# A mixture of experts with a residual on one core: block products of 4x4 in place of 2x2 in 52 of 72 units

## The chip, the core and the metric

The kernel runs on one core of a Trainium2 chip (trn2). The metric is the device time of one execution in microseconds. All data is fp32.

## The reference

The input x has 16 batch rows of 256 tokens with 256 features. Eight experts and one shared expert each have two matrices up (Wg, Wu, 256 x 1024) and one down (Wd, 1024 x 256). Cut to what matters:

```python
g = jnp.einsum('bsd,edf->ebsf', h, Wg)
u = jnp.einsum('bsd,edf->ebsf', h, Wu)
expert_outs = jnp.einsum('ebsf,efd->ebsd', jax.nn.silu(g) * u, Wd)
expert_output = jnp.einsum('be,ebsd->bsd', gating_probs, expert_outs)
shared = jnp.einsum('bsf,fd->bsd', jax.nn.silu(h @ Sg) * (h @ Su), Sd)
sg = shared_gate_prob[:, :, None]
out = x + (1.0 - sg) * expert_output + sg * shared
```

## The kernel before, in words

**Units.** The work is cut into 72 units: for each expert (the shared one is the ninth), for each half of the 1024 hidden features, for each group g of four batch rows. The loop at the end of the kernel goes through them in this order, so four units follow each other with the same weights. A unit computes a 4x4 grid of hidden blocks (four chunks of 128 features against four batch rows of 256 tokens), for the gate (m = 0) and for the up matrix (m = 1).

**Up.** Products are saved by algebra. Four diagonal blocks are computed plainly (`diagonal`, two weight halves each: the bank D, the copies p and q in SBUF). For each of the six pairs i < j of `PAIRS`, three products give both off-diagonal blocks (`offdiagonal`): one of summed weights and summed x goes to a bank M; GpSimd makes s from q and p (lines 281, 285 on are the helpers `tt` and `stt`); VectorE puts M + s into a bank X as a seed; two more products are added onto X by TensorE. The bank is then consumed: ScalarE applies silu for the gate (line 643), VectorE multiplies the up bank by the gate and by the coefficient of expert and batch row, in one scalar_tensor_tensor per block (`mult`), into a tile h. Summed weights come from `load_base` and `make_pair`, the x sums (xp, xd) were kept in HBM at the start and are loaded again for every unit by SP (line 276).

**Down.** `unit_down` sees the h blocks as 2x2 blocks and uses seven products instead of eight, for each of two feature halves f, which are added in the bank: 14 matmuls of 512 columns. It needs six sums of h by VectorE and two by GpSimd (`sum_`), and sums of Wd from `load_down`. ScalarE copies each of the seven banks dn into a tile ev (line 765), and two DMAs of GpSimd's queue add four and three of these into `total[g]` in HBM (line 780; without adding in the first round, line 778). At the end `load_pieces` and `finish` join the seven pieces of each group into the output, with transposes (line 866); the last unit goes down plainly (`last_down`).

**Order.** Every operation is given to a plan (`add`) with an engine, a length, a rank and the tiles that it makes and uses. A unit takes 12 ranks. `Plan.run` plays the whole program through once when the kernel is built: on each engine the ready operation of lowest rank goes first, tiles are handed out from the list of their tag, and TensorE's operations keep the order of rank within each of two streams (dn or not). The instructions are emitted in the order found, each engine's in a fixed order. PSUM has eight banks: three X, two M, one D, two dn.

## Time and profile before

| what | value |
|---|---|
| median of 3 runs | 2527.62 us (2527.4 to 2527.68) |
| the profiled execution | 2527.65 us |
| its span, first to last instruction | 2525.9 us |
| TensorE busy | 2512.4 us (99%), 9637 matmul records |
| VectorE, ScalarE, GpSimd busy | 1850.4, 788.1, 1718.6 us |
| granted TensorE clock | 1.000 |
| moved by DMA | 425.18 MB, 168 GB/s |

Engines in the profile are PE (TensorE), PEld (its weight loads, which overlap it), DVE (VectorE), ACT (ScalarE), POOL (GpSimd) and SP (SyncE). A group line gives the line of the kernel, engine, operation, written tile <- read tiles, shapes and count; then busy time and mean duration in ns; then the idle time of the engine just before these instructions, and what ended it. L281 is the helper for all two-tensor operations, L545 that for all matmuls, so groups are told apart by their tiles. An fp32 matmul appears as two records. Some 100 us at each end, where tables are made and pieces joined, differ from the steady middle.

### The profile page before, as it was taken

Reading aid. Unit: us, or ns where it says so; the run is one execution under the profiler, and the core shown is the slowest. Engines: PE = TensorE matmul, PEld = TensorE weight load, DVE = VectorE, ACT = ScalarE, POOL = GpSimd, SP = SyncE. Lnnn points to the kernel's source line nnn. Section 1 sums busy time; section 2 is a strip of 40 time slices with the busy share of each in tenths; the row PEclk is TensorE's granted clock in tenths of the full one; section 3 lists DMA queues with packets and bytes.
Section 4 is the critical chain, followed back from the end, with each engine's and each line's share of the span. In section 5 each row is a group of like instructions: output and inputs, shape, how many; then the busy total and the mean of one; then the engine's idle time right before and its main releaser. Section 6 shows DMA issues by size and latency. Waiting matters only on the chain. (4 is left out here: it accounts for less than half of the span.)

```text
span 2525.9 us, 30304 instructions
## 1 busy us (share of the span) xinstructions
PE 2512.4 (99%) x9637; PEld 1817.6 (72%) x9637; DVE 1850.4 (73%) x3246; ACT 788.1 (31%) x1389; POOL 1718.6 (68%) x1652
## 2 busy tenths in 40 slices
PE   9999999999999999999999999999999999999999
PEld 5767777777777777777777777777777777777776
DVE  7896767677776768676767767677767777776787
ACT  3333333333333333333333332333332333332321
POOL 7686767676676767676766667576767676676664
PEclk9999999999999999999999999999999999999999
DMA  7545666566666566666666666665666665666566
GB/s 258 181 163 158 172 161 177 158 167 159 170 161 177 157 155 163 163 169 169 166 159 166 163 169 168 162 155 155 175 161 177 157 167 157 175 160 156 153 191 202
DMA packets 179666, 425.18 MB, mean 168 GB/s; under 512 B 15120, under 2 KB 84256, under 8 KB 170544
## 3 DMA queue, kind: packets, MB, share of 16 engines
q1 hardware_dynamic: 158224, 294.18, 35.3%
q0 software_dynamic: 20224, 128.53, 27.0%
q8 instruction: 76, 1.25, 0.2%
q14 instruction: 86, 0.70, 0.1%
q10 hardware_dynamic: 1056, 0.52, 0.1%
HBM read 276.90 MB, written 146.28 MB: 168 GB/s over the span
## 5 line engine op out<-in xcount | busy, mean ns | idle before, releaser
L281 POOL TENSOR_TENSOR s<-pq,pq 128x512 f32<-128x512 f32 x852 | 1134.6, 1360 | 518.8 <-DVE X L281 507.7
L545 PE MATMUL dn<-h,wd 128*128 128x512 f32 x1988 | 1013.8, 592 | 0.4 <-DVE ev L281 0.4
L545 PE MATMUL X<-xp,wp 128*128 128x256 f32 x3408 | 875.5, 379 | 3.6 <-DVE X L281 3.5
L281 DVE TENSOR_TENSOR X<-M,s 128x512 f32<-128x512 f32 x852 | 588.8, 693 | 365.8 <-PE M L545 236.6
L545 PEld LDWEIGHTS X<-xp,wp 128*128 128x128 f32 x3408 | 646.4, 190 | 238.0 <-issue 123.8
L545 PE MATMUL D<-xd,wb 128*128 128x256 f32 x2272 | 583.8, 379 | 1.1 <-ACT sg L643 0.8
L286 DVE SCALAR_TENSOR_TENSOR h<-X,coef,sg 128x256 f32<-128x256 f32 x852 | 397.9, 478 | 244.5 <-PE X L545 190.2
L545 PEld LDWEIGHTS M<-xp,wp 128*128 128x128 f32 x1704 | 323.4, 190 | 316.8 <-issue 301.3
L545 PE MATMUL M<-xp,wp 128*128 128x256 f32 x1704 | 506.8, 379 | 0.0
L765 ACT COPY ev<-dn 128x512 f32<-128x512 f32 x490 | 287.5, 587 | 635.5 <-PE dn L545 635.5
L545 PEld LDWEIGHTS D<-xd,wb 128*128 128x128 f32 x2272 | 430.9, 190 | 66.2 <-issue 3.0
L281 DVE TENSOR_TENSOR h<-h,h 128x512 f32<-128x512 f32 x426 | 454.7, 1093 | 0.0
L545 PEld LDWEIGHTS dn<-h,wd 128*128 128x128 f32 x1988 | 377.5, 190 | 56.3 <-issue 4.3
L572 ACT COPY pq<-D 128x512 f32<-128x512 f32 x284 | 166.2, 585 | 413.0 <-PE D L545 386.5
L643 ACT ACTIVATE sg<-X 128x512 f32<-128x512 f32 x434 | 258.4, 595 | 115.6 <-PE X L545 106.4
L643 ACT ACTIVATE sg<-D 128x512 f32<-128x512 f32 x142 | 84.8, 597 | 525.5 <-DVE pq L281 525.5
L281 DVE TENSOR_TENSOR pq<-D,pq 128x256 f32<-128x256 f32 x568 | 222.0, 415 | 34.8 <-PE D L545 34.3
L780 POOL DMA_DIRECT2D total<-ev x132 | 116.6, 883 | 186.1 <-ACT ev L765 176.9
L281 POOL TENSOR_TENSOR h<-h,h 128x512 f32<-128x512 f32 x142 | 199.4, 1404 | 49.3 <-PE dn L545 31.6
L281 POOL TENSOR_TENSOR wp<-wb 128x128 f32<-128x128 f32 x216 | 140.4, 685 | 0.0
L286 DVE SCALAR_TENSOR_TENSOR h<-D,coef,sg 128x256 f32<-128x256 f32 x284 | 134.4, 474 | 0.0
L281 POOL TENSOR_TENSOR wp<-wp,wb 128x256 f32<-128x256 f32 x108 | 81.8, 764 | 1.3
(73 smaller groups left out, 470.7 us busy)
## 6 DMA issues: line engine op xcount, KB each, us to landing
xp<-keep_p SPq DMA_DIRECT2D x408, 384.0 KB, 4.0
total<-ev POOLq DMA_DIRECT2D x70, 1024.0 KB, 9.2
xd<-keep_d SPq DMA_DIRECT2D x136, 512.0 KB, 3.5
total<-ev POOLq DMA_DIRECT2D x70, 768.0 KB, 6.7
wb<-in_L_cond_Wg_dram SPq DMA_DIRECT2D x32, 256.0 KB, 9.9
wb<-in_L_cond_Wu_dram SPq DMA_DIRECT2D x32, 256.0 KB, 5.2
wd<-in_L_cond_Wd_dram SPq DMA_DIRECT2D x64, 128.0 KB, 4.0
keep_p<-xp SPq DMA_DIRECT2D x18, 384.0 KB, 3.4
```

Source lines behind the costliest of these rows:

```text
L281: return add(engine, length, rank, lambda: eng.tensor_tensor(o(), a(), b(), op), deps, new, uses)
L286: lambda: nc.vector.scalar_tensor_tensor(o(), a(), c() if callable(c) else c, b(), ALU.mult, op),
L545: lambda: nc.tensor.matmul(o(), w(), mv(), start=start, stop=stop, skip_group_check=onto),
L572: lambda: nc.scalar.copy(p_[:, 2 - 2 * a : 4 - 2 * a, :], bank[:, :, :]), ps,
L643: lambda: nc.scalar.activation(b[:, :, :], bank[:, :, :], AF.Silu), deps, [b], [bank],
L765: lambda ev=ev, at=at, bank=bank: nc.scalar.copy(ev[:, at, :], bank.tile.rearrange("p a t -> p (a t)")),
L780: nc.gpsimd.dma_start(total[g][part], ev[:, 0:k, :], accum_op=ALU.add)
```

## The change

Units 4 to 55 go down by another scheme; the first 4 and the last 16 keep the 2x2 blocks.

- **Down by 4x4 blocks.** The four chunks of features and the four batch rows are treated as in the way up, with Wd as the third matrix (m = 2) of `load_base` and `make_pair`. Each of the six pairs gives three products, and eight more belong to the diagonal: 26 of 256 columns, two in each of 13 banks dn. ScalarE copies the 13 banks to ev, and four DMAs (of 3, 3, 3 and 4 banks) add them to a second set of sums in HBM, `star_total`.
- **What it needs.** For each pair, VectorE multiplies the up bank by the gate in place, ScalarE copies it to h, and VectorE adds both blocks to two places each of a tile acc (8 x 256 columns, one instruction of 1024) and sums the two blocks into g. ScalarE starts acc from the two diagonal tiles. The coefficient now goes into the gate by ScalarE (`scale`, two of 256 columns per gate).
- **Both M products of a pair share one bank** in units 4 to 71; a fourth bank serves X in units 4 to 55.
- **Merge.** In the last 16 units, four `merge` calls, one per group, load the sums of `star_total`, combine them on VectorE with a PSUM bank T and ScalarE, and add four blocks to `total`.
- **Memory handed over.** Three tiles of 8 x 256 serve first as 12 tiles h, in the middle as two acc and one more ev, then as h again (`plan.shift`); likewise wd becomes wp and g, and xio becomes wb.
- **The plan.** Ranks come from a table `RANK`; lengths of VectorE and GpSimd operations that share a port are laid end to end; GpSimd's constant in a length goes from 0.3 to 0.17.

The functions of before live on as `unit_up_w`, `unit_down_w` and `offdiagonal_w` (the last used in the first four units only). The core of the diff:

```diff
@@ -20,11 +20,24 @@
+
+
+RANK = {
+    "first": 4, "q": 2.6, "dc": 2.45, "acc": 0.3, "g": -5.1, "cp": 1.6, "seed": -0.05, "s": -2.0,
+    "lagx": 1.5, "sc": 6.1, "bank": (6.6, 7.1, 8.6, 15.9, 16.4, 16.9, 17.3), "ev": 0.55, "p": 1.8, "xc":
+    0.7, "st": -3.8, "qa": -2.25, "da": 0.25, "ga": -3.25, "pace": 3, "m0": -0.6, "m1": 3.25, "xm": 0,
+    "w": 16, "mp": 8, "m2": 1.5, "ml": 1.75, "lagw": 1.25, "wp": 0.05, "wq": 0.6, "wqa": 0, "wdc": 1.45,
+    "ws": 1.0, "wseed": 0.2, "wxc": 1.7, "to": (-12, 6, -6, -19, -34), "back": (0, 72, -6, -33, 4, 80,
+    20),
+}
+
...
@@ -208,20 +262,50 @@
     banks = tags("X", [P, 2, TB], 3, psum)
-    tags("M", [P, 2, TB], 2, psum)
+    mbanks = tags("M", [P, 2, TB], 2, psum)
     tags("D", [P, 2, TB], 1, psum)
     tags("dn", [P, 2, TB], 2, psum)
+    tags("T", [P, 2, TB], 0, psum)
...
     tags("wb", [P, 4, 2, P], 4)
     tags("wp", [P, 3, P], 16)
-    tags("wd", [P, 2, 7, P], 2)
     tags("pq", [P, 4, TB], 8)
     tags("s", [P, 2, TB], 3)
     tags("sg", [P, 2, TB], 5)
-    tags("h", [P, 2, TB], 22)
+    tags("h", [P, 2, TB], 10)
     tags("ev", [P, 4, 2 * TB], 2)
-    tags("xio", [P, 2, D], 4)
+    tags("g", [P, TB], 0)
...
+        ] if m < 2 else None
         late = 0 if rank < 0 else 8
         ru, rv = ranks or (rank, rank)
+        if m == 2:
+            rows = sources(e)[2][ts(half, 4 * P), :].rearrange("(c p) (k q) -> p c k q", p=P, q=P)
         engine = "ACT" if ranks and m == 0 else "SP"
-        u = load(ru, lambda: b[:, :, 0, :], src[0], 256, [], [b], late=late, engine=engine)
-        v = load(rv, lambda: b[:, :, 1, :], src[1], 256, [], [], [b], late=late)
+        if m == 2:
...
+
+    FIRST, LAST = RANK["first"], NE * NHALF * NG - RANK["w"]
+
+    def star(n):
+
+        return FIRST <= n < LAST
 
...
-    def offdiagonal(n, m, unit, k, rank, pq, pqops, consume):
+    def offdiagonal(n, unit, k, rank, pqs, pqops, consume):
+
+        e, half, g = unit
+        i, j = PAIRS[k]
+        xb, xo = xp[g, k], xpop[g, k]
+        mb = Buf("M", f"M_{n}_{k}")
+        m1 = []
+        for m in range(2):
+            w, wo = pair[m, e, half, k], pairop[m, e, half, k]
+            m1.append(
+                mm(
+                    MM, rank + m / 100, lambda m=m: mb[:, m, :], lambda w=w: w[:, 0, :], lambda: xb[:, 0, :],
+                    m == 0, True, m == 1, [wo, xo[0], *m1], [mb] if m == 0 else [], [w, xb] if m == 0 else [w, xb, mb],
+                )
+            )
+        for m in range(2):
+            w, wo = pair[m, e, half, k], pairop[m, e, half, k]
+            p_, q_ = pqs[m]
+            s, xbank = Buf("s", f"s_{m}_{n}_{k}"), Buf("X", f"X_{m}_{n}_{k}")
+            so = tt(
+                "POOL", rank + m - (RANK["s"] if star(n) else RANK["ws"]), lambda s=s: s[:, :, :], lambda q_=q_: q_[:, i : j + 1 : j - i, :],
+                lambda p_=p_: p_[:, 3 - j : 4 - i : j - i, :], ALU.subtract, 2 * TB, [pqops[m][i], pqops[m][j]],
+                [s], [p_, q_],
+            )
+            seed = tt(
+                "DVE", rank + m + (RANK["seed"] if star(n) else RANK["wseed"]), lambda xbank=xbank: xbank[:, :, :],
+                lambda m=m: mb[:, m : m + 1, :].broadcast_to([P, 2, TB]), lambda s=s: s[:, :, :], ALU.add, 2 * TB,
+                [so, *m1], [xbank], [mb, s], False,
+            )
+            m67 = [
+                mm(
+                    MM, rank + m + (LAGX if star(n) else RANK["lagw"]) + (3 + h) / 8, lambda xbank=xbank, h=h: xbank[:, h, :],
+                    lambda w=w, h=h: w[:, 2 - h, :], lambda h=h: xb[:, 2 - h, :],
+                    False, True, True, [seed, wo, xo[2 - h]], [], [xbank, w, xb],
+                )
+                for h in range(2)
+            ]
+            consume[m](xbank, m67, rank + m + (LAGX + RANK["xc"] if star(n) else RANK["lagw"] + RANK["wxc"]), [(j, i), (i, j)])
...
+        def scale(b, h, block, rank, deps):
+            return add(
+                "ACT", act(TB), rank,
+                lambda: nc.scalar.mul(b[:, h, :], b[:, h, :], coef[:, e, 4 * g + block : 4 * g + block + 1]),
+                [*deps, coef_op], uses=[b],
+            )
+
...
+                ops = [op]
+                if True:
+                    ops = [scale(b, h, block, rank + RANK["sc"], [op]) for h, (_, block) in enumerate(which)]
+                    if key[0] == "d":
...
+            op = add(
+                "DVE", dve(4 * TB), rank, lambda: nc.vector.tensor_tensor(view(), view(), twice(), ALU.add),
+                [*deps, *state["acc"]], [], [acc, *uses], port=port,
+            )
+            state["acc"] = [op]
+
...
+        def start_acc(a, b, deps, rank):
+
+            ops = [
+                add(
+                    "ACT", act(2 * TB), rank, lambda: nc.scalar.mul(acc[:, 2 - 2 * a : 4 - 2 * a, :], b[:, :, :], -1.0),
+                    deps, [acc] if state["new"] else [], [b] if state["new"] else [b, acc],
+                )
+            ]
+            state["new"] = False
...
+                ops.append(
+                    add(
+                        "ACT", act(TB), rank, lambda h=h: nc.scalar.copy(acc[:, 5 + 2 * a - h, :], b[:, h, :]),
+                        [*deps, ops[0]], [], [b, acc],
+                    )
+                )
+            state["acc"] += ops
+
+        def sum_pair(k, rank, b, x, deps, uses, port):
+            gb = Buf("g", f"g_{n}_{k}")
+            op = tt("DVE", rank, lambda: gb[:, :], x, lambda: b[:, 1, :], ALU.add, TB, deps, [gb], [b, *uses], port)
+            pairs[k] = (gb, op)
+
...
+                op = tt(
+                    "DVE", rank, lambda: bank[:, :, :], lambda: bank[:, :, :], lambda: sg[:, :, :], ALU.mult, 2 * TB,
+                    [*deps, *sgops], [], [bank, sg], False,
+                )
+                c = add(
+                    "ACT", act(2 * TB), rank + RANK["cp"], lambda: nc.scalar.copy(b[:, :, :], bank[:, :, :]), [op], [b], [bank]
+                )
+                for h, at in enumerate(which):
+                    hb[at] = (b, h, c)
+                acc_pair(k, rank + RANK["acc"], lambda: bank[:, :, :], [c], [bank], False)
+                sum_pair(k, rank + RANK["g"], b, lambda: bank[:, 0, :], [c], [bank], False)
+
+            return consume
+
+        pqs = {m: (Buf("pq", f"p_{m}_{n}"), Buf("pq", f"q_{m}_{n}")) for m in range(2)}
+        pqops = {0: {}, 1: {}}
+        for d in range(4):
+            a, m = d // 2, d % 2
+            pqops[m].update(
+                diagonal(n, m, unit, a, r0 - W + 3 * d, pqs[m], (gate(f"d{a}"), up(f"d{a}", None))[m])
+            )
+        for k in range(len(PAIRS)):
+            offdiagonal(n, unit, k, r0 + 2 * k, pqs, pqops, (gate(f"o{k}"), up(f"o{k}", k)))
+        return hb, pairs, acc, state
...
+    def unit_down(n, unit, hb, pairs, acc, state):
+        e, half, g = unit
+        r0 = W * n
+        work = []
+        for k, (i, j) in enumerate(PAIRS):
+            w, wo = pair[2, e, half, k], pairop[2, e, half, k]
+            gb, go = pairs[k]
+            hbuf, h, ho = hb[i, j]
+            lo = [ho, hb[j, i][2]]
+            work.append((lambda w=w: w[:, 0, :], wo, lambda gb=gb: gb[:, :], [go], [w, gb]))
+            work.append((lambda w=w: w[:, 1, :], wo, lambda hbuf=hbuf: hbuf[:, 1, :], lo, [w, hbuf]))
+            work.append((lambda w=w: w[:, 2, :], wo, lambda hbuf=hbuf: hbuf[:, 0, :], lo, [w, hbuf]))
+        w, (u, rops) = base[2, e, half], baseop[2, e, half]
+        for at in range(8):
+            i, part = (3 - at, 0) if at < 4 else (at - 4, 1)
+            work.append(
+                (lambda i=i, part=part: w[:, i, part, :], rops[i] if part else u, lambda at=at: acc[:, at, :],
+                 state["acc"], [w, acc])
+            )
+        ev, evops = None, []
+        for b in range(13):
+            part, at = (b // 3, b % 3) if b < 9 else (3, b - 9)
+            rank = r0 + (BANK[b % 3] + 4 * (b // 3) if b < 9 else BANK[b - 6])
+            bank = Buf("dn", f"dn_{n}_{b}")
+            ops = []
+            for h in range(2):
+                wv, wo, mv, mo, bufs = work[2 * b + h]
+                ops.append(
+                    mm(
+                        MM, rank + h / 100, lambda bank=bank, h=h: bank[:, h, :], wv, mv, h == 0, True, h == 1,
+                        [wo, *mo, *ops], [bank] if h == 0 else [], bufs if h == 0 else [*bufs, bank],
+                    )
+                )
+            if at == 0:
+                ev, evops = Buf("ev", f"ev_{n}_{part}"), []
...
+
+                def store(ev=ev, part=part, first=first, k=k):
+                    if first:
+                        nc.gpsimd.dma_start(star_total[g][part], ev[:, 0:k, :])
+                    else:
+                        nc.gpsimd.dma_start(star_total[g][part], ev[:, 0:k, :], accum_op=ALU.add)
+
+                starop[g, part] = add(
+                    "POOL", 0.9, rank + 0.4, store, [*evops, starop.get((g, part))], uses=[ev],
+                    lag=3.0, kb=256 * k * (1 if first else 1.8),
+                )
+
+    BANK = RANK["bank"]
+
...
+    def merge(g, rank):
...
+        view, by, ops = load_sums(g, rank - 2.5)
+        for k, (i, j) in enumerate(PAIRS):
...
+            y = [
+                tt(
+                    "DVE", r, lambda at=at: view(4 + at), lambda at=at: view(4 + at), lambda h=h, bank=bank: bank[:, h, :], op, TB,
+                    [cp, *ops], [], [by, bank], False,
+                )
+                for at, h, op in ((i, 1, ALU.add), (j, 0, ALU.subtract))
+            ]
+            c = tt(
+                "DVE", r, lambda tv=tv: tv(0), lambda tv=tv: tv(0), lambda bank=bank: bank[:, 0, :], ALU.subtract, TB,
+                [cp], [], [t, bank], False,
+            )
+            c = tt(
+                "DVE", r, lambda bank=bank: bank[:, 0, :], lambda tv=tv: tv(0), lambda bank=bank: bank[:, 1, :],
+                ALU.subtract, TB, [c, *y], [], [t, bank], False,
+            )
+            z = stt(
+                r, lambda i=i, j=j: by.tile[:, 3 - j : 4 - i : j - i, :], lambda bank=bank: bank[:, 0:1, :].broadcast_to([P, 2, TB]),
+                -1.0 / d, lambda i=i, j=j: by.tile[:, 3 - j : 4 - i : j - i, :], ALU.add, 2 * TB, [c, *ops], [], [by, bank], False,
+            )
+            ops = [*y, z]
+        for i, t in enumerate(POINTS):
+            if t:
+                ops = [
+                    stt(r, lambda i=i: view(4 + i), lambda i=i: view(3 - i), float(t), lambda i=i: view(4 + i), ALU.add, TB, ops, [], [by]),
...
@@ -931,7 +1350,12 @@
             for k in range(len(PAIRS)):
                 for m in range(2):
                     make_pair(m, e, half, k, r0 + 2 * k + m - (8 if n else -4))
-            load_down(e, half, r0 + W - 8)
+            if not star(n):
+                load_down(e, half, r0 + W - 8)
+            else:
+                load_base(2, e, half, r0 - 3)
+                for k in range(len(PAIRS)):
+                    make_pair(2, e, half, k, r0 + 2 * k + 1)
         if n == end:
...
-        hb, hops = unit_up(n, unit)
+        if star(n):
+            unit_down(n, unit, *unit_up(n, unit))
+            continue
+        for k in range(NG):
+            if n == LAST + int(RANK["m0"] + RANK["m1"] * k + RANK["m2"]):
+                merge(k, W * (LAST + RANK["m0"] + RANK["m1"] * k))
+        hb, hops = unit_up_w(n, unit)
...
+    r0, r1 = W * FIRST, W * LAST
+    bank("M", "X", r0 - 0.01, 1)
+    bank("X", "T", r1 + RANK["xm"], 0)
+    for k, (tag, view) in enumerate((("acc", big_acc[0]), ("acc", big_acc[1]), ("ev", big_ev[2]))):
+        plan.shift([(r0 + RANK["to"][k], "h", big_h[k])], [(tag, [view])])
+        plan.shift([(r1 + (RANK["back"][k] if k != 1 else W * (RANK["m0"] + 3 * RANK["m1"]) + 14), tag, [view])], [("h", big_h[k])])
+    plan.shift([(r0 + RANK["to"][3], "wd", low_wd[:1])], [("wp", low_wp[0]), ("g", low_g[0])])
+    for k in range(2):
+        plan.shift(
+            [(r1 + RANK["back"][3], "wp", low_wp[k]), (r1 + RANK["back"][4 + 2 * k], "g", low_g[k])], [("wd", [low_wd[k]])]
+        )
+    plan.shift([(r0 + RANK["to"][4], "xio", side_xio)], [("wb", side_wb)])
+    plan.shift([(r1 + RANK["back"][5], "wb", side_wb)], [("xio", side_xio)])
     last = {}
```

## The prediction

> **What bounds the kernel now.** I began with the busy time of the whole span and of its steady part, 200 to 2400 us. Columns of the second view: stretch, length, then busy us (and instructions) of each engine, granted clock, DMA share, GB/s.
>
> ```profile
> PE 2512.4 (99%) x9637; PEld 1817.6 (72%) x9637; DVE 1850.4 (73%) x3246; ACT 788.1 (31%) x1389; POOL 1718.6 (68%) x1652
> ```
> ```profile
> 200.00:2400.00 2200.00, 2199.80 (x8425) 1600.33 (x8424) 1582.79 (x2806) 696.00 (x1215) 1497.01 (x1427) 1.00 0.63 164
> ```
>
> TensorE is never idle at full clock. As a busy TensorE need not be at its peak, I then looked at its pace in the timeline (start, duration). What counts is the distance of the starts.
>
> ```profile
> 1200.86 1.03 PE L545 MATMUL D<-xd,wb 128*128 128x256 f32 x4
> 1201.73 1.03 PE L545 MATMUL X<-xp,wp 128*128 128x256 f32 x4
> 1202.59 1.02 PE L545 MATMUL dn<-h,wd 128*128 128x512 f32 x2
> 1203.45 0.59 PE L545 MATMUL M<-xp,wp 128*128 128x256 f32 x2
> ```
>
> Four records of 256 columns take 0.86 us, two of 512 as well. The groups show two records for each fp32 product (3408 X records / 71 units = 48 for 24 products), so a 256-column product costs 0.43 us and a 512-column one 0.86. A unit has 52 small products up (16 D, 12 M, 24 X) and 14 large ones down: 80 in small ones, 80 x 0.43 = 34.4 us. The real period: the accumulating DMAs of total run from 213.3 (unit 4, first) to 2471.9 (unit 69, second), the two of a unit 14.2 apart, so 65 periods are 2244.4 us, 34.53 each. Only 0.13 us a unit is lost; time is the count of products.
>
> Then the groups, for what the other engines pay (idle time left aside; "busy, mean ns"):
>
> ```profile
> L281 DVE TENSOR_TENSOR X<-M,s 128x512 f32<-128x512 f32 x852 | 588.8, 693 | 365.8 <-PE M L545 236.6
> L286 DVE SCALAR_TENSOR_TENSOR h<-X,coef,sg 128x256 f32<-128x256 f32 x852 | 397.9, 478 | 244.5 <-PE X L545 190.2
> L281 DVE TENSOR_TENSOR h<-h,h 128x512 f32<-128x512 f32 x426 | 454.7, 1093 | 0.0
> L281 DVE TENSOR_TENSOR pq<-D,pq 128x256 f32<-128x256 f32 x568 | 222.0, 415 | 34.8 <-PE D L545 34.3
> L765 ACT COPY ev<-dn 128x512 f32<-128x512 f32 x490 | 287.5, 587 | 635.5 <-PE dn L545 635.5
> L281 POOL TENSOR_TENSOR s<-pq,pq 128x512 f32<-128x512 f32 x852 | 1134.6, 1360 | 518.8 <-DVE X L281 507.7
> ```
>
> In the steady part (2200 / 34.53 = 63.7 units) a unit has DVE 24.8, ACT 10.9, POOL 23.5 us busy. Last, what DVE waits for there (total, times, longest) and the DMA queues over the span:
>
> ```profile
> DVE X L281 <- PE M L545: 225.2, 220, 2.3
> DVE h L286 <- PE X L545: 183.0, 161, 1.9
> DVE X L281 <- issue: 54.7, 66, 1.3
> DVE X L281 <- POOL s L281: 41.3, 33, 1.3
> ```
> ```profile
> q1 hardware_dynamic: 158224, 294.18, 35.3%
> q0 software_dynamic: 20224, 128.53, 27.0%
> ```
>
> Most of DVE's idle time is waiting for TensorE, which costs nothing. The fences show where the change can bite: DVE, ACT and the DMA engines.
>
> **What the Trainium skill says.** VectorE: DVE Perf Modes, section "The TRN2 errata — SBUF-src ops pay a fixed extra latency per instruction": an fp32 tensor_tensor takes (N+151)/0.96 ns, 691 at N=512; the trace has 693. It prices N=1024, which the trace lacks, at 1224 ns. SBUF — State Buffer, section "Who interferes with whom": a DVE instruction with two SBUF inputs contends with GpSimd reads, one with at most one does not. The trace agrees: h<-h,h (two SBUF inputs) means 1093 ns, X<-M,s of equal size 693. DMA: Bandwidth & Descriptors, section "Issuing engines are not separate DMA queues": all queues end on the same 16 engines and interleave. The trace agrees: 35.3% and 27.0% make the 0.63 of the steady part.
>
> **TensorE, the gain.** Units 4 to 55 (52 of 72) keep the 52 products up. Down, 13 banks of two 256-column products replace 14 large ones: 26 for 28, 78 x 0.43 = 33.54 us. Two products fewer in 52 units: 52 x 0.86 = **44.7 us**, the ceiling. Weight loads: 156 a unit of 190 ns instead of 132; the X rows already keep a pace of 0.215 us a record with one load each, so I add nothing.
>
> **DVE.** Per 4x4 unit: 12 seeds 8.29 (588.8/71), 8 q 3.13 (222.0/71), 8 products with the gate at 0.693 (nearest row: X<-M,s) 5.54, 6 acc additions of 128x1024 with one PSUM input 7.34 (the page's price; low end four times the slope 693-415=278 ns, 1.11 each; high end 1.97, if they paid the 1093/693 of contention), 6 pair sums at 0.40 2.4 (q row: 0.39 busy, 0.415 mean), weights 106.0/71 x 1.5 = 2.24 (wb and wp rows; three matrices for two). Sum 28.9. Gone are the h sums (6.4) and 16 products with coef. The same rows of before sum to 26.8 where the windows show 24.8, since neighbours overlap; so 26.7 to 28.9 of 33.54, **80 to 86%** after 72%. With acc at its ends the sum is 28.2 to 33.4.
>
> **ACT.** Evictions 13 x 0.587 = 7.6, gates 4.8 (343.2/71), D copies 2.3, 16 scales by coef at 0.417 (the xp scaling row) 6.7, 6 copies of X 3.5, two 512-wide negations at 0.63 (0.417 plus the slope 0.587-0.376) 1.3, four 256-wide copies 1.7. Sum 27.9 of 33.54, **83%** after 31%. Back-to-back ones overlap by 0.1 (gates at 1215.03 and 1215.53 of 0.60 each), so 24 is the low end.
>
> **POOL.** 12 s at 1.27 to 1.36: 15.2 to 16.3; four DMA issues at 0.88: 3.5 instead of 1.8; weight sums (222.2+38.8)/71 x 1.5 = 5.5 instead of 3.7 and 0.8 for wd; h sums (2.8) gone. Sum 24.2 to 25.3, 75%; s queues behind DMA issues that wait for ACT's last eviction of a part, as now (170 us in the steady part), twice as often. The DVE work left has a PSUM input almost throughout, so s should fall to its undisturbed 1.27: nothing added.
>
> **DMA.** Accumulation grows from 7 to 13 blocks of 256 KB a unit. Rate now: 128.53 MB in 27.0% of 2525.9 us, 188 GB/s; 13 x 0.262 MB = 18.1 us. Plain traffic 4.09 MB a unit at 330 GB/s (294.18 in 35.3%): 12.4. Together 30.5 of 33.54, 91%; at the 200 and 355 GB/s of the densest stretches (211 at a share of 1.01 from 1218 us, 373 at 1.05 from 20 us) 28.5, 85%. On SP's queue only the load of down weights changes, one of 512 KB for four of 128 KB. A part is due every 8.4 us, three ev buffers give each 25 us; filling needs about 6, landing 6.7 to 9.2 now. I take no cost.
>
> **The last 16 units and the seams.** Both M products share one bank, the counts are unchanged. Four merges: per merge six pairs of 4 DVE sums at 0.415 and one 512-wide at 0.756 (478+278), three 0.82 and one 1.09: 18 us, in all 72 us of DVE, 4 x 4.4 of ACT, loads of 3.3 MB each, four POOL issues each. What hides them is DVE's idle 34.53-24.8 = 9.7 us a unit, 155 us in 16 units; without that cover they cost up to 72. I take 1.5. At the second seam unit 55 goes down within itself and 56 only in the next period: one stretch has 52 products (22.4 us) against 20.4 of DVE work (8.3+5.6+1.9+3.1+1.5); I take 2, range 0 to 5. The first seam stacks TensorE work instead. Its bank hand-over issues one zero matmul, under 0.5 us.
>
> **Sum.** Against the profiled execution, 2527.65 (span 2525.9 and 1.75 around it; median of the runs 2527.62, so no shift): -44.7, +1.5, +2, and for fuller queues 0.06 us a unit on top of today's 0.13, +3: 2527.65 - 38 = **2490**. What is late next is still TensorE.
>
> **Rivals.** *B, bursts take half.* ACT at 83% delays evictions of the two dn banks (the last four banks of a unit are due within 1.4 ranks, 4 us); TensorE stalls 0.35 to 0.9 us a unit beyond the sum: 2505 to 2533. For it: ACT's load grows 2.5 times; against: evictions need 0.59 of the 0.86 that a bank's products take.
> *C, DVE becomes the bound.* Of its idle 9.7 us, waits not put down to TensorE are about 2.6 us (POOL 69, ACT 41, issue 56 over 63.7 units). New waits arise: each product now waits for ACT's scaling, each acc addition for ACT's copy, and behind a waiting DVE instruction stand seeds for which TensorE waits. With 28.9 busy it decides from 34.53-28.9 = 5.6 us of such idle. At 6.6 a unit takes 35.5: +1 x 52 = 52, so 2580. Against: only 80% busy if neighbours overlap, and seeds lead the X products by 1.5 ranks (4 us).
> *D, the DMA engines become the bound.* Decides from (34.53-12.4)/13 = 1.70 us a block, against 1.39 now; at the 2.5 us between the landings of 1024 and 768 KB (9.2, 6.7) a unit takes 45 us, +540. Against: those landings shared the engines with plain loads.
> *E,* that fewer products don't save, is excluded by the pace.
>
> **Chances.** Forecast, 2480 to 2505: 0.60. B as a gain, 2505 to 2522: 0.12; as no change: 0.06. C 0.16, D 0.06. A run can tell about 0.2%, 5 us. So faster 0.72, same 0.06, slower 0.22. The range runs from the ceiling and a little (2480) into C, to 2545; about 0.16 lies above, little below. The forecast's own range is 2480 to 2505.
>
> **What would show it.** Right: units 33.6 to 33.8 us apart, TensorE 99%, acc additions near 1.22 us, s near 1.27, DVE 80 to 86%. B: weight loads or products into dn waiting for ACT evictions. C: products into X waiting for seeds, TensorE under 97%. D: waits for xp or xd loads, landings of ev over 19 us. I am wrong if 4x4 units exceed 34.2 us.

## The result and the profile after

The changed kernel takes 2538.31 us (median of 5 runs, 2535.15 to 2540.82) against 2527.62: 1.0041 times the time of before, 95% interval 1.0027 to 1.0056. Slower by 0.4%, where 1.5% faster was forecast. The profiled execution took 2535.15 us. Ratios here and below are against the kernel before, timed again on the same chip beside each experiment (2527.62 to 2527.88 us).

First the views that answer to those of before: busy time, the steady stretch (length, busy us and instructions of PE, PEld, DVE, ACT, POOL, then clock, DMA share, GB/s), and TensorE's pace.

```profile
PE 2486.8 (98%) x10885; PEld 2057.6 (81%) x10886; DVE 2051.4 (81%) x3330; ACT 1570.7 (62%) x3185; POOL 1698.7 (67%) x1759
```
```profile
200.00:2400.00 2200.00, 2167.47 (x9641) 1833.25 (x9640) 1778.17 (x2882) 1458.72 (x2969) 1474.54 (x1525) 1.00 0.83 209
```
```profile
1200.85 1.03 PE L640 MATMUL D<-xd,side 128*128 128x256 f32 x4
1201.71 1.03 PE L640 MATMUL X<-xp,wp 128*128 128x256 f32 x4
```

TensorE computes 26 us less and keeps the old pace, 0.86 us for four records of 256 columns. But before it was hardly ever idle in this stretch (2199.80 of 2200 us), and now it is for 32.5 us (2200 - 2167.47). Where? The chain of work that ended last (start, duration) shows the same place in every unit:

```profile
414.36 1.73 PE dn L640 x8
...
450.43 1.73 PE dn L640 x8
...
484.10 1.73 PE dn L640 x8
```

The distances are **36.07** and 33.67, and 33.67 again for the units ahead of these. In the kernel before, the four D records that start at 1200.86 in the prediction's timeline have these as their counterpart one unit later:

```profile
1235.33 1.03 PE L545 MATMUL D<-xd,wb 128*128 128x256 f32 x4
```

So an undisturbed 4x4 unit takes 33.67 us, 0.79 less than the 34.46 of before (the mean over the steady middle); but one unit in four, where the weights change, loses time, 2.40 us here. What TensorE waits for from 200 to 1980 us (total, times, longest):

```profile
PE dn L640 <- DVE low L365: 22.4, 11, 2.1
```

low is here a tile g, the sum of a pair's two blocks, that the last products down need. The timeline at one of the eleven stops (start, duration, engine; in brackets the idle time before it and what ended it):

```profile
438.03 0.87 POOL L1111 DMA_DIRECT2D star<-ev  x1 [0.74 <-ACT ev L1097]
...
438.63 1.17 POOL L365 TENSOR_TENSOR wp<-side 128x128 f32<-128x128 f32 x2
...
439.47 2.77 POOL L365 TENSOR_TENSOR s<-pq,pq 128x512 f32<-128x512 f32 x2
...
441.07 3.62 DVE L370 SCALAR_TENSOR_TENSOR low<-side,low 128x256 f32<-128x256 f32 x1
...
443.43 0.97 POOL L365 TENSOR_TENSOR wp<-wp,side 128x256 f32<-128x256 f32 x1
...
444.95 0.41 DVE L365 TENSOR_TENSOR low<-X,h 128x256 f32<-128x256 f32 x1
...
445.41 0.70 PE L640 MATMUL dn<-low,wp 128*128 128x256 f32 x2 [2.13 <-DVE low L365]
```

Line 370 with two SBUF inputs, one instruction of a weight sum, stands on VectorE for 3.62 us: until GpSimd pauses (GpSimd's last instruction ends at 444.40, this one at 444.69). Behind it stand a copy q and the sum g; behind g stands TensorE.

Two more losses. The granted clock falls to half after some stops (same columns as above; the clock is the third number from the end):

```profile
174.80:178.20 3.40, 3.40 (x8) 2.48 (x9) 3.40 (x6) 1.37 (x3) 3.28 (x4) 0.50 0.88 306
1133.90:1140.70 6.80, 5.95 (x15) 4.72 (x15) 4.83 (x8) 3.64 (x7) 3.27 (x3) 0.50 0.00 0
```

With three more such stretches (3.4 us each from 1550.3, 1826.8 and 2045.3) that is 20.4 us at half clock, so 10.2 us lost; before had none. And at the first seam, where the 4x4 units begin, VectorE has no pause at all, while a product M waits 3.2 us for it:

```profile
166.00:177.00 11.00, 7.82 (x27) 5.42 (x26) 11.00 (x14) 3.77 (x8) 11.00 (x11) 0.90 0.39 108
```

The balance of the profiled executions, in us; idle is span less busy, and "at full clock" is busy less half of the time at half clock. The last two columns are experiments told below.

| | before | after | pool_turns | issue_turns |
|---|---|---|---|---|
| span | 2525.9 | 2533.4 | 2487.1 | 2495.1 |
| TensorE busy | 2512.4 | 2486.8 | 2473.9 | 2477.2 |
| of it at half clock | 0 | 20.4 | 6.8 | 13.6 |
| TensorE at full clock | 2512.4 | 2476.6 | 2470.5 | 2470.4 |
| TensorE idle | 13.5 | 46.6 | 13.2 | 17.9 |

After against before: -35.8 of work, +10.2 of half clock, +33.1 of idle time, +7.5 in all. The change does save its products; stops take back more than that.

The other groups, waits and queues that the prediction spoke of (group lines: busy, mean ns, idle before):

```profile
L895 DVE TENSOR_TENSOR big<-big,X 128x1024 f32<-128x1024 f32 x235 | 284.0, 1209 | 0.0
L859 ACT ACTIVATE sg<-sg,coef 128x256 f32<-128x256 f32 x832 | 385.3, 510 | 2.2
L1097 ACT COPY ev<-dn 128x512 f32<-128x512 f32 x458 | 268.0, 586 | 188.4 <-PE dn L640 182.8
L365 POOL TENSOR_TENSOR s<-pq,pq 128x512 f32<-128x512 f32 x852 | 1131.3, 1368 | 497.6 <-DVE X L365 359.8 <-DVE M L365 128.8 <-PE D L640 6.6
L370 DVE SCALAR_TENSOR_TENSOR wp<-wb,wp 128x256 f32<-128x256 f32 x75 | 90.1, 1204 | 0.0
```
```profile
DVE low L365 <- ACT h L943: 85.3, 92, 2.0
```
```profile
q0 software_dynamic: 39552, 214.52, 42.8%
```

The acc addition costs 1209 ns, close to the 1224 priced; ACT's evictions still wait for TensorE, not the other way round; VectorE's longest waits are now for ScalarE's copies h, which do not decide: pool_turns, below, has them too and no stop; GpSimd's queue of DMAs went from 27.0% to 42.8%. But s did not get faster (1368 ns), and the weight sum wp rose to 1204 ns from 724 in the groups of before.

### The profile page after: what moved, and what is told of

Same layout as the page of the kernel before. It is cut to its first block, busy times and chain, and to the rows that moved or that the text cites. A ratio compares the mean times of both kernels' runs of the same rounds, so it can differ in the third digit from the quotient of the medians.

```text
span 2533.4 us, 34723 instructions
## 1 busy us (share of the span) xinstructions
PE 2486.8 (98%) x10885; PEld 2057.6 (81%) x10886; DVE 2051.4 (81%) x3330; ACT 1570.7 (62%) x3185; POOL 1698.7 (67%) x1759
## 3 DMA queue, kind: packets, MB, share of 16 engines
q0 software_dynamic: 39552, 214.52, 42.8%
## 4 chain that ended last, share of the span: by engine, by line
PE 93%; DVE 4%; issue 1%; DMA 0%; ACT 0%; SPq 0%; DVEq 0%; ACTq 0%
PE dn L640 31%; PE M L640 22%; PE X L640 21%; PE D L640 19%; DVE X L365 1%; DVE pq L365 1%; DVE wp L370 1%; DVE big L365 0%; DVE wb L365 0%; DMA wb<-in_L_cond_Wg_dram 0%; DVE h L365 0%; DVE low L365 0%; DVE h L370 0%; PE dn L1285 0%; DVE M L365 0%
## 5 line engine op out<-in xcount | busy, mean ns | idle before, releaser
L365 POOL TENSOR_TENSOR s<-pq,pq 128x512 f32<-128x512 f32 x852 | 1131.3, 1368 | 497.6 <-DVE X L365 359.8
L365 DVE TENSOR_TENSOR X<-M,s 128x512 f32<-128x512 f32 x630 | 427.0, 692 | 120.8 <-PE M L640 75.0
L640 PE MATMUL X<-xp,wp 128*128 128x256 f32 x2004 | 522.9, 380 | 1.1 <-DVE X L365 1.0
L640 PEld LDWEIGHTS X<-xp,wp 128*128 128x128 f32 x2004 | 380.9, 190 | 94.5 <-issue 39.8
L859 ACT ACTIVATE sg<-sg,coef 128x256 f32<-128x256 f32 x832 | 385.3, 510 | 2.2
L895 DVE TENSOR_TENSOR big<-big,X 128x1024 f32<-128x1024 f32 x235 | 284.0, 1209 | 0.0
L640 PE MATMUL dn<-h,wp 128*128 128x256 f32 x976 | 274.2, 380 | 0.0
L365 DVE TENSOR_TENSOR X<-X,sg 128x512 f32<-128x512 f32 x235 | 163.3, 695 | 78.8 <-ACT sg L859 39.7
L640 PE MATMUL dn<-h,low 128*128 128x512 f32 (+1 forms) x554 | 217.3, 489 | 0.1
L640 PEld LDWEIGHTS dn<-h,wp 128*128 128x128 f32 x976 | 185.6, 190 | 26.5 <-ACT ev L1097 0.8
L365 DVE TENSOR_TENSOR M<-M,s 128x512 f32<-128x512 f32 x222 | 153.5, 691 | 41.2 <-PE M L640 27.2
```

Source lines behind the costliest of these rows:

```text
L365: return add(engine, length, rank, lambda: eng.tensor_tensor(o(), a(), b(), op), deps, new, uses, port=port)
L640: lambda: nc.tensor.matmul(o(), w(), mv(), start=start, stop=stop, skip_group_check=onto),
L859: lambda: nc.scalar.mul(b[:, h, :], b[:, h, :], coef[:, e, 4 * g + block : 4 * g + block + 1]),
L895: "DVE", dve(4 * TB), rank, lambda: nc.vector.tensor_tensor(view(), view(), twice(), ALU.add),
```

## The experiments

The theory after the comparison: **the port**, a name for the contention of which the prediction speaks. VectorE's weight instruction with two SBUF inputs waits for GpSimd, and a run of GpSimd instructions passes it over. The rivals: the longer chain of the 4x4 scheme (scaling, copy, g) is simply late; or the rebuilt plan of all units costs time.

**1. pairs_act.** The second half of a pair's weight sum goes to ScalarE and GpSimd, which have room, instead of VectorE.

```diff
-        elif e == half == 0:
+        elif True:
             o = add(  # ACT multiplies, GpSimd subtracts; was one DVE stt
```

> Theory (port): in the group-change units the weight instruction of VectorE with two SBUF inputs (wp<-wb,wp) stands still as long as GpSimd's instructions follow each other without a gap, and the sum g behind it makes TensorE wait 2.1 us. Here ScalarE scales and GpSimd subtracts instead, so VectorE has no such instruction in the weight sums of pairs. Expected: the stops of 1.6 to 2.1 us at dn<-low in every fourth unit vanish, TensorE idle from 42 to under 20 us, clock back to 0.998 or more, 2500 us (2495 to 2510), although GpSimd gets 9 x 0.73 us more in each group. Rival (GpSimd is overloaded where the weights change): its added work makes those units longer, 2540 or more. Rival (VectorE has too much work there, blocked or not): a gain too, since 9 instructions are gone, but of at most half, 2518 to 2525.

Measured: 2513.08 us, ratio 0.9941 (0.9926 to 0.9955), just above the expected 2495 to 2510. The stops for g are gone with the weight instruction, which points to it; but the plan was drawn up anew here, so the order changed too. And another stop came in each group of four units: the next instruction with two SBUF inputs, `load_base`'s sum of only 128 columns, now stands 4.46 us, and TensorE waits 0.9 us for a gate behind it, 11 times. Its timeline, again with a DMA issue of GpSimd ahead:

```profile
418.97 0.87 POOL L1111 DMA_DIRECT2D star<-big  x1 [0.83 <-ACT big L1097]
...
421.86 4.46 DVE L370 SCALAR_TENSOR_TENSOR wb<-wb 128x128 f32<-128x128 f32 x1
```

**2. pool_waits.** VectorE keeps its instruction, but GpSimd's first subtraction of the next pair waits for it, so GpSimd has to pause there.

```diff
+    held = [[], [], []]
...
-            [rops[i], rops[j]], [b], [w],
+            [rops[i], rops[j], *held[m][-1:]], [b], [w],
...
+            held[m].append(o)
```

> The same instructions as the changed kernel on every engine; only, the first GpSimd subtraction of a pair waits until VectorE's weight sum of the pair before (of the same matrix) is done, so GpSimd pauses. Theory (port): VectorE's instruction gets through at the pause, is blocked for one or two GpSimd instructions at most; the stops shrink by more than half, 2505 to 2520 us. Rival (too much work on VectorE in these units): same work, so the stops stay, 2533 to 2540. Rival (GpSimd overloaded): the pauses make it worse, over 2540.

Measured: 2508.19 us, ratio 0.9924 (0.9908 to 0.9941). All work is still there, yet no stop for g is left in the groups: four units take 4 x 33.76 us. That speaks against the first rival but does not settle it. The plan took the new wait into account, so VectorE's instructions stand in another order (at 1154 of 3330 places). And the long waits are still there: 15 of VectorE's 128x256 weight sums took over 2.3 us from 200 to 1980 us, as many as in the changed kernel, but TensorE no longer needed what stood behind them. Experiment 5 keeps the order.

**3. no_star.** All 72 units as in the last 16 of the changed kernel, by 2x2 blocks, with the changed plan.

```diff
-    "first": 4, ...
+    "first": 72, ...
-    "w": 16, ...
+    "w": 0, ...
...
```

> No unit goes down by 4x4 blocks, no merge, no memory handed over: the first kernel's scheme in all 72 units with the changed plan (port, lengths, order). Theory: the plan's changes and the rest cost nothing by themselves, 2527 us (2524 to 2530), TensorE idle about 8 us. Rival (the new order is worse for the 2x2 units, which would explain what the first and last units lost): 2532 or more.

Measured: 2527.29 us, ratio 0.9998 (0.9989 to 1.0006). In 2x2 units the new plan, the shared bank of M and the lengths cost nothing; the second rival falls. (The last lines of the edit, left out here, hand the shared tiles to the 2x2 units from the start.)

**4. first8.** The 4x4 units begin at unit 8 instead of 4, away from the change of weights (`"first": 8`).

> The 4x4 units begin at unit 8 in place of 4 (48 of them). Theory: unit 5 lost 7.3 us (41.5 in place of 34.2) because the x sums (xp, xd, made with two SBUF inputs) of the last groups and the weight sums meet there on VectorE and GpSimd; at unit 8 no x sums are made, so the seam costs 1 to 2 us, and one group less saves 0.8 less: 2530 us (2527 to 2532). Rival (the hand-over of memory and banks costs it, wherever it lies): as the changed kernel, 2535 to 2541.

Measured: 2568.7 us, ratio 1.016 (1.0145 to 1.0175), where 2527 to 2532 was expected: a clear miss. The stop of the seam is gone, but the order of each group shifts, and its stops grow: from 200 to 1980 us TensorE waits 25.7 us for g, up to 3.0 at a time, and 7.6 for gates.

What the port costs hangs on which instruction meets which run of GpSimd.

**5. pool_turns.** The same instructions, on every engine in the same order as in the changed kernel, for the waits are added after the plan has run; but after each VectorE instruction on the port (the kernel marks these operations, `op.port`), GpSimd's next one on the port waits for it.

```diff
+            if op.port and op.engine == "DVE":
+                pending = ins.name
+            elif op.port and op.engine == "POOL" and pending:
+                tc.add_manual_dep(ins, pending, port_wait, reason="port")
+                pending = None
```

> The changed kernel with its instructions and its order; only, after every VectorE instruction with two SBUF inputs the next GpSimd sum in the plan's order waits until it is done. Theory (port): so the order that the plan assumed on the port holds everywhere, at the seams and in the merges too: TensorE idle 10 to 18 us, no VectorE instruction of 128x512 or less over 2.2 us, clock 0.999 or more, 2493 us (2487 to 2502), at least 6 below the kernel in which only the pair sums do so (2508). Rival (what was left there, the first seam with 4.4 us idle and the last 16 units, is too much work for VectorE, not the port): no better than 2505.

Measured: **2489.14 us** (2488.1 to 2489.49), ratio 0.9847 (0.9832 to 0.9861): faster than both kernels. The timeline at the place shown above:

```profile
441.14 0.41 DVE L370 SCALAR_TENSOR_TENSOR low<-side,low 128x256 f32<-128x256 f32 x1
...
441.63 1.28 POOL L365 TENSOR_TENSOR s<-pq,pq 128x512 f32<-128x512 f32 x1 [0.54 <-PE X L640]
441.81 0.42 DVE L365 TENSOR_TENSOR low<-X,h 128x256 f32<-128x256 f32 x1
```

0.41 instead of 3.62 us; GpSimd starts this s 0.9 us later than in the changed kernel (441.63 for 440.69), g is done at 442.2 instead of 445.4, and TensorE does not stop. Nearly every unit takes 33.67 us (33.69 on average). A chain that was simply late would have stayed late in this unchanged order, so here the first rival falls. Five VectorE instructions still take over 2.3 us (3.12 at most), where the changed kernel has 28.

**6. no_star_turns.** The same waits in no_star, the control.

> The 2x2 scheme in all 72 units, with the same waiting of GpSimd for VectorE. There VectorE's h sums are blocked too (2.4 us in every unit of the kernel before), but TensorE waited for none of it. Theory: the same time, 2527 us (2523 to 2530), since each unit already takes its 34.46 us of products; the port matters only where the slack is gone. Rival (the blocked port also cost the kernel before): under 2522. Rival (GpSimd's waits cost by themselves): over 2531.

Measured: 2524.33 us, ratio 0.9987 (0.998 to 0.9994): 3 us less than no_star, against 49 us with the 4x4 units. The waits repair what the change brought; they are no general gain.

**7. first8_turns.** Both edits.

> As the kernel whose 4x4 units begin at unit 8, with GpSimd waiting for each VectorE instruction with two SBUF inputs. Theory (port): all that the later start lost (2568.7 against 2538.3) was blocked VectorE instructions, in an order that happened to fall worse; with the waits it comes to 2489 plus 3.1 for one group less, minus up to 5 for the first seam's stop (3.0 us idle, and half clock for 6.8 us), so 2488 (2485 to 2494). Rival (the later start is worse for another reason, such as the tiles handed over later): over 2500.

Measured: 2499.88 us, ratio 0.9888 (0.9872 to 0.9905), between the theory's 2485 to 2494 and the rival's 2500. Of first8's excess of 79.5 us over pool_turns the waits remove 68.8; 3 more follow from four units fewer with 4x4 blocks (4 x 0.79), and 4.5 are stops in the last 16 units. The rest stays open.

**8. How long does GpSimd keep the port? Three benchmarks.** In the changed kernel VectorE's instruction stood through four GpSimd instructions at the place shown above, and through up to seven elsewhere. These kernels hold none of the model; they put VectorE additions of 128x256 beside rows of GpSimd additions. The first: one at the start of rows of 2 to 16.

> Not the model: copies x to the output and leaves out all experts; it times one VectorE addition of 128x256 beside a row of GpSimd additions of 128x512. Theory (port): with two SBUF inputs it lasts until the row of 2, 4, 8 or 16 GpSimd instructions has ended, about 2.5, 5, 10 and 20 us, not one GpSimd instruction (1.3); with one input in PSUM it takes 0.4 us beside 8 of them; where the third or fifth GpSimd instruction waits for it, it ends after two or four, about 2.6 and 5.1 us. Rival (the port is handed over at each instruction): 1.3 to 1.7 us in all rows. Rival (GpSimd slows any VectorE instruction): the PSUM one takes as long as the others.

The tile's view (durations in ns: least/median/most):

```profile
L84 DVE TENSOR_TENSOR f<-g,e x18: 1466/1468/2689, 7.7 to 223.5; 128x256 f32<-128x256 f32 x18
L84 DVE TENSOR_TENSOR f<-g,bank x3: 420/420/422, 49.9 to 201.2; 128x256 f32<-128x256 f32 x3
```

With a PSUM input 0.42 us. With two SBUF inputs 1.47 us, whatever the length of the row: it waits for the running addition only. (The 2.69 are the rows whose third GpSimd addition itself waits for VectorE.) "It waits for the whole row" falls. The second benchmark varies the arrival in eight steps and the width of GpSimd's additions:

> Not the model: copies x to the output and leaves out all experts; one VectorE addition of 128x256 with two SBUF inputs beside ten GpSimd additions, of 128 columns, then 256, then 512, arriving at eight times. The first such measurement showed it passed over by one GpSimd instruction in 3 of 21 rows only, not by whole rows. Theory A (short GpSimd instructions, queued ahead, keep the port): at 128 columns it is passed over by several, 2 us or more, at 512 it waits for the running one only, 0.4 to 1.5 us. Theory B (it depends on the moment of arrival): the durations within one width differ by more than one GpSimd instruction. Theory C (neither; what passes it over in the model is something else, such as GpSimd's instructions that wait for semaphores): at every width at most the running instruction and its own 0.4 us.

The durations are 0.42 to 1.36 us, never more than one GpSimd addition and its own; at two of the 24 arrivals, 0.03 to 0.04 us ahead of a GpSimd start, that next one went first. The third has two VectorE additions per row and mixed widths:

> Not the model: copies x to the output and leaves out all experts. Two VectorE additions of 128x256 with two SBUF inputs beside one row of eight GpSimd additions, with a VectorE addition in PSUM of rising length between them; rows of 512 columns, then rows that mix 512, 256 and 128 as where the weights change. In the changed kernel the instructions that were passed over by up to five began beside a GpSimd instruction of 1.55 to 1.60 us, one that had itself been held up (1.27 undisturbed). Theory D: once VectorE has held up GpSimd, GpSimd's next instructions are queued ahead and keep the port, so the second addition lasts 2 us or more in most rows, the first 1.47 at most. Rival (the port is handed on at each boundary, as in the measurement with one addition): the second also takes at most the running GpSimd instruction and its own 0.4 us, under 1.7, but for single rows.

```profile
L84 DVE TENSOR_TENSOR f<-e,o x16: 911/1144/1377, 10.3 to 152.5; 128x256 f32<-128x256 f32 x16
```

This is the second of a row; the first took 1.47 us always. Again one instruction each. So far the benchmarks contradicted the model, and something of the model was missing in them.

**9. port_bench4.** All 28 VectorE operations of over 2.3 us in the changed kernel, and all 68 in the kernel before, stand in a run of GpSimd without a pause in which a DMA issue came ahead of them (as the first of the run in 20 and 65 cases). So the benchmark got one: eight rows as before, eight with a plain DMA issued by GpSimd just ahead of the row, eight with an accumulating one.

```diff
         pool_op(g, f, b)
+        if kind == 1:
+            put(lambda: nc.gpsimd.dma_start(far[k], src))
+        elif kind == 2:
+            put(lambda: nc.gpsimd.dma_start(far[k], src, accum_op=ALU.add))
```

> A microbenchmark, not the model; its output is not the model's. 24 rows on GpSimd: two 128x512 additions, then ten more back to back (two of 512 columns, eight of 256). Beside each row VectorE makes one 128x256 addition of two SBUF inputs that arrives during the third addition, at eight arrival times. The first eight rows are as in the benchmarks before; in the next eight GpSimd issues a 512 KB DMA right before the row; in the last eight that DMA also adds in place. In the model VectorE's long waits began after such an issue, with GpSimd's records 0.3 us into each other in place of 0.04. Theory E (after an issue GpSimd's instructions are queued ahead and keep the port until it pauses): 1.5 us in the first eight rows, over 3 us in most of the other sixteen, with GpSimd's records overlapping by about 0.3 us there. Rival (an issue leaves no trace on the port): 1.5 us in all 24 rows, perhaps one addition more in single rows; then what lets GpSimd keep the port over several instructions in the model stays open.

The tile's view of the three stretches (no issue; plain; accumulating), one after the other:

```profile
L84 DVE TENSOR_TENSOR f<-e,o x8: 897/1130/1358, 11.4 to 93.9; 128x256 f32<-128x256 f32 x8
```
```profile
L84 DVE TENSOR_TENSOR f<-e,o x8: 1319/6291/6522, 105.9 to 192.6; 128x256 f32<-128x256 f32 x8
```
```profile
L84 DVE TENSOR_TENSOR f<-e,o x8: 7502/7732/7965, 204.7 to 294.5; 128x256 f32<-128x256 f32 x8
```

And one row with an accumulating issue in the timeline (x10 are ten additions end to end):

```profile
226.72 0.85 POOL L97 DMA_DIRECT2D far<-src  x1
227.33 1.54 POOL L81 TENSOR_TENSOR o<-a,b 128x512 f32<-128x512 f32 x1
...
229.77 8.12 POOL L81 TENSOR_TENSOR o<-a,b 128x512 f32<-128x512 f32 x10
...
230.35 7.83 DVE L84 TENSOR_TENSOR f<-e,o 128x256 f32<-128x256 f32 x1
```

After an accumulating issue the same addition stands to the end of the row, at all eight arrivals. After a plain one it is passed over by seven GpSimd additions at six of the eight arrivals, and gets in, without a pause of GpSimd, before the row is over (at the other two it is passed over by one and by none). So an issue earlier in a run can turn a wait for one instruction into a wait for most or all of the run. In the model an issue is needed for this but does not decide alone. From 200 us on, of the changed kernel's VectorE instructions with two SBUF inputs, none of the 138 that started in a run of GpSimd without an issue was passed over by another GpSimd instruction, and 30 of the 101 in a run with one were; in the kernel before, 1 of 251 and 66 of 73. One part of the expectation failed: the starts that lie 0.3 us inside the instruction before are seen only after the accumulating issue (the additions at 227.33 and 228.56 take 1.54 and 1.52); after a plain one the overlap is 0.04 us as without, and the port is kept all the same.

**10. issue_turns.** Back in the model: only the first VectorE instruction on the port after each DMA issue gets its turn. The edit is shown against pool_turns.

```diff
-    pending = None
+    pending, armed = None, False
...
+            if op.engine == "POOL" and op.kb:
+                armed, pending = True, None
-            if op.port and op.engine == "DVE":
+            elif op.port and op.engine == "DVE" and armed and not pending:
                 pending = ins.name
             elif op.port and op.engine == "POOL" and pending:
+                armed = False
...
```

> The changed kernel with fewer of the waits that gave 2489.1: only after each DMA that GpSimd issues, the next VectorE instruction on the port has its turn, that is, GpSimd's next instruction on the port waits for it; 357 waits in place of 1041. In the changed kernel all 28 VectorE instructions of over 2.3 us stand in an unbroken run of GpSimd that began with such an issue. Theory E (the issue puts GpSimd in a state in which it keeps the port until it pauses, and one turn ends that state): 2487 to 2494, no regular stop of TensorE from 200 to 1980 us. Rival (the issue is a chance companion of busy stretches, or one turn does not end the state, and all the turns are needed): 2497 to 2515, with some of the stops at weight changes left.

(The counts in this text are three times too high: it is 119 waits in place of 347. And the run began with the issue in 20 of the 28 cases; in the others the issue came later in it.) Measured: 2493.87 us, ratio 0.9864 (0.9848 to 0.9881), with no stop for g from 200 to 1980 us. A third of the waits brings 44 of the 49 us. The rest is half clock and idle time, mostly in the last 16 units (table above).

## Why the prediction was wrong, point by point

**The step that failed** is in the part on POOL: "The DVE work left has a PSUM input almost throughout, so s should fall to its undisturbed 1.27: nothing added." Most of VectorE's time does go to work with a PSUM input, but s stayed at 1368 ns, and the little that is left on the port decides: the prediction put the waiting for it at nothing, and removing most of it (pool_turns) was worth 49 us, half clock behind the stops included: as much as the whole miss (2538 against 2490). The weight sums were entered as "106.0/71 x 1.5 = 2.24" us a unit, a mean. They do not come in every unit: they come in one of four, in a row, on a GpSimd that has issued a DMA and runs on without a pause. There 0.41 us can become 3.62, with a finished product behind them in the queue. Eleven such stops make 22.4 of the 33.1 us of new idle time.

The warning was in the profile of before: the tile's view of h (ns: least/median/most).

```profile
L281 DVE TENSOR_TENSOR h<-h,h x426: 674/794/3708, 55.0 to 2483.3; 128x512 f32<-128x512 f32 x142
```

I read its mean of 1093 as a mild slowdown of each; but half of them take under 0.85 us, and 64 of the 426 over 2.3. TensorE did not wait then: it was idle for 0.2 us of the steady part. The Trainium skill puts the lock more strongly than I used it: SBUF — State Buffer, section "SBUF: two separate sides", says that the port is "an **exclusive lock**, not a bandwidth split", and that whichever instruction starts first has it for its whole length. The benchmarks without an issue agree (1.47 us beside one addition of 1.27); behind an issue the measurement decides otherwise: the waiting instruction took 3.62 us in the model and up to 7.97 in the benchmark, far more than one GpSimd instruction and its own 0.4.

**DMA issues of GpSimd** were priced at their own time, "four DMA issues at 0.88: 3.5 instead of 1.8". They cost no time on GpSimd that mattered. But issue_turns and port_bench4 show that an issue can put the port out of VectorE's reach for the rest of a run of GpSimd, and the change doubles them in 52 units.

**The seams.** "The first seam stacks TensorE work instead" failed: VectorE has no pause there (in the kernel before it has none in this stretch either, but TensorE waited only 0.5 us for it), and TensorE lost 3.2 us, and 1.7 in the half clock that followed. In pool_turns this stop remains (3.0 us, then 6.8 us at half clock), so turns on the port do not cure it; beginning at unit 8 does (first8). Which of VectorE's work there comes too early was not tried. The second seam and the merges, entered with 2 and 1.5 us, cost about 0.65 us of idle time in pool_turns.

**The half clock** was not in the sum: 10.2 us. Trainium skill, TensorE: Matmul & The Clock Gate, section "What's actually happening", ties half clock to an idle window of about 3.4 us; the stretches here last 3.4 or 6.8 us, but they came after stops of 1.6 to 3.2 us, and at only some of them. Why at these was not tried.

**The saving** had its mechanism right and its size a little high: "52 x 0.86 = 44.7". Measured, 34.46 - 33.67 = 0.79 a unit, 41. (The 34.53 of the prediction, from DMA issues far apart, is 0.07 too long for the steady middle.) Since 156 records of 256 columns take 33.67, one takes 215.8 ns; 104 of these and 28 of 512 columns took 34.46, so one of those took 429.1, which is 2.5 ns less than two short ones. The cost per record is what the same page of the skill gives in its section "Wait — 56ns, not 53.3ns?", about 2.5 ns; 24 more records a unit cost 0.06 us.

**What held.** The view of the stretch with 4x4 units, same columns as before:

```profile
200.00:1980.00 1780.00, 1752.90 (x8063) 1533.13 (x8062) 1425.04 (x2236) 1316.17 (x2719) 1169.25 (x1236) 1.00 0.84 211
```

"Units 33.6 to 33.8 us apart": 33.67 where undisturbed, though with the stops four units average 34.27, over the 34.2 that I had named as the mark of being wrong. DVE 80 to 86%: 1425.04 of 1780 us, 80%, and in pool_turns, with less waiting for the port in it, 78%. acc at 1224 ns: 1209. (Its high end, 1.97, should have been 1.93: 1.224 x 1093/693. It decided nothing.) DMA: share 0.84 for 85 to 91% and no wait of TensorE for a transfer in the groups, so rival D was rightly set low. ACT 83%, at its low end 72%: 74%, though its scaling costs 0.510 us and not 0.417. Its evictions did not hold TensorE up (B). POOL 75% was too high: 66%.

**The rivals.** C had the sign, and one clause of its mechanism: what stands "behind a waiting DVE instruction". It expected a VectorE with too little idle time; VectorE was 80% busy as forecast, and too late at one point in four units.

That pool_turns lands on 2489.14, next to the forecast 2490, is partly luck. The rest of the sum was sound to a few us a term, but the errors cancel: a saving 4 too high and some 6 us for the first seam's stop and half clock, against 3 of fuller queues and nearly 3 of second seam and merges that did not come, and up to 3 that the turns gain in 2x2 units too (no_star_turns). About 6 us of after's busy time stay unplaced (2476.6 against 2470.5 at full clock); the modelled ends of matmuls hide part of each stop, 2.40 of period against 2.13 of idle time at 445 us.

## What to carry to other kernels

Read a slow group by its least, median and most, not by its mean, and ask what stands in the queue behind the slowest. Where GpSimd issues DMAs and then computes without a pause, a VectorE instruction with two SBUF inputs may wait through most or all of that run; one dependency that makes GpSimd wait after each issue was worth 44 us here. And a mean over units hides work that falls into one of them.

## What the runs showed of the hardware that was not expected

- One 128x256 VectorE addition of two SBUF inputs beside a row of twelve GpSimd additions: 0.9 to 1.4 us without a DMA issue ahead, 7.5 to 8.0 behind an accumulating issue, 6.2 to 6.5 behind a plain one at six of eight arrivals.
- In the changed kernel no VectorE instruction was passed over (0 of 138) in a run of GpSimd without an issue, and 30 of 101 were in a run with one. Why the other 71 got through, and what the issue leaves behind inside GpSimd, was not tried.
- One wait of GpSimd after an issue was enough to remove the regular stops. Whether GpSimd's pause or VectorE's turn ends what the issue begins was not separated; behind a plain issue VectorE got in before any pause.
- Stops of TensorE of 1.6 to 3.2 us were followed by 3.4 or 6.8 us at half clock in some places (five in after) and not in others.
